# Two attention layers: packed third block for layer 2's keys and queries, shared image values for pairs of entries in layer 1

## The chip, the cores and the metric

The kernel runs on one core of a Trainium2 chip. The core has a matrix engine (PE, with its weight loads shown apart as PEld), a vector engine (DVE), a scalar engine (ACT), a general engine (POOL) and a queue engine (SP) that here issues nearly all DMAs. The metric is the device time of one execution in microseconds (us); lower is better. A profiled execution gives besides a trace of every instruction, whose times count from the first instruction (the span).

## The reference, cut to what matters

Sixteen entries (B = 16) of 256 query tokens with 320 channels pass through two cross-attention layers. Each attends to 256 context tokens of 512 channels. In layer 1 the first 77 are text and the other 179 are image tokens; in layer 2 the last 4 are image tokens and 252 are text. There are 20 heads of 16 channels.

```python
# layer 1 (layer 2 alike, with text = all but the last 4, and image scores by head)
text, ip = ctx[:, :77], ctx[:, 77:]
q, k_text, v_text = x @ Wq, text @ Wk, text @ Wv
logits = einsum("bhqd,bhkd->bhqk", heads(q), heads(k_text)) * scale
text_out = softmax(logits) @ heads(v_text)
ip_k, ip_v = ip @ Wk_ip, ip @ Wv_ip
scores = einsum("bhqd,bhkd->bhqk", heads(q), heads(ip_k)) * scale
...
ip_probs = softmax(scores + 0.5 * sem) * spatial_mask
out = (text_out + ip_probs @ heads(ip_v)) @ Wout + bout + x
```

## The kernel before, in words

**Numbers.** Every f32 operand is split into a high half, which the matrix engine takes exactly, and a low half, the remainder. `prod` (L255) makes a product of two split operands from three matmuls for each 128 rows of contraction: high by high, high by low, low by high. With 512 context channels that is 4 x 3 = 12 matmuls for one output block.

**Stages.** Layer 1 runs in 80 slots (16 entries x 5 groups of 4 heads; `slot0`, L810), then layer 2 in 80 slots (`slot1`, L993). A slot makes the scores of the group two ahead, the exponentials of its own and the weighted values of the group before. Between these stand fillers: the work of other entries (context, keys, queries, values, output projections), each a generator whose steps have a due time in slots in the table `STEPS` (L1186); `fill` (L1161) runs those that are due. PE follows the order in which this code issues in both layers; ACT, DVE and POOL do so in layer 2 and are put in order by the framework's scheduler in layer 1, as SP is in both.

**Keys and queries of layer 2.** `keys1` (L553) makes the keys in three blocks of 128 columns, `queries` (L636) with `project` (L626) the queries. There are 320 columns, so the weights are padded to 384 (24 columns for the 20 heads) and half of the third block is padding. High and low halves go to DRAM (`kd[1]`, `qd`) in three planes: for the keys low, high, high; for the queries high, low, high. `stacks1` (L747) loads them back for two heads at a time as stacks of 3 x 16 = 48 rows (`XROW`) on partitions 0 and 64 of the tiles `ks` and `qs`, so that one matmul with 48 rows of contraction makes all three products of a head's scores. Row 48 is used for the maximum that is subtracted (`KS1` = 49 rows). The loads are issued four slots ahead (`LEAD`), the scores made two slots ahead (`both1`, L903).

**Values of layer 1.** `values0_` (L423) makes, for each entry, three blocks of 128 tokens by 320 channels: t = 0, the text values of tokens 0 to 127; t = 1, the image values of the same tokens; t = 2, the image values of tokens 128 to 255. Of t = 0 and t = 1 the rows that don't belong are multiplied by zero when ACT moves the result to the value tile (`vr`, a ring of three, L429). In block t = 1 only the last 51 rows (tokens 77 to 127) count. The context of two entries is loaded and split together (`ct0`; tiles `cta` and `ctb`). `attend0` (L803) multiplies the value tiles with the probabilities.

**Order around the change.** SP issues in order: a DMA that waits holds up all that stand behind it. In layer 1 the stacks of a group can be loaded when PE is done with the group four before. In layer 2 the first stack of an entry waits for the keys' last block (`keys_out`, L347).

## Time and profile before

| | |
|---|---|
| median of 3 runs | 1475.77 us (1475.01 to 1476.06) |
| the profiled execution | 1477.49 us |
| its span, first to last instruction | 1475.7 us |
| PE busy | 1433.6 us (97%), 12438 matmuls |
| weight loads | 1186.7 us (80%) |
| DVE / POOL / ACT busy | 1166.0 (79%) / 1151.8 (78%) / 956.5 us (65%) |
| DMA | 211.78 MB, mean 144 GB/s |
| layer 1's scores, first to last | 44.0 to 645.9 us |
| layer 2's scores, first to last | 659.4 to 1430.4 us |

A row of the group list reads: line, engine, operation, what it writes and reads by the program's names, shapes, number, then busy time and the mean of one in nanoseconds, then the engine's idle time just before. A row of a timeline: start, duration, engine, line, operation. Matmuls overlap, so that the duration of one is longer than what it adds; what it adds is the distance to the next one's start. Issuing a DMA does not count as busy time; SP's issues stand in its timeline as SPq.

### The profile page before, as it was taken

What the parts mean: (1) busy time and instruction counts of PE and PEld (TensorE: products, weight loads), DVE (VectorE), ACT (ScalarE), POOL (GpSimd) and SP (SyncE); (2) the same over time, 40 slices, a digit from 0 to 9 for tenths busy, and PEclk for the clock granted to TensorE, in tenths of its full rate; (3) what the DMA queues carried; (4) which work ended last, traced back from release to release, by engine and by line L of the source; (5) the groups of instructions that cost most, each with busy time, mean ns of one, the idle gap of its engine ahead of it and who ended that gap; (6) DMA issues with size and microseconds to landing.
All of it is one profiled execution on the core that took longest, in us unless ns stands there. A gap on an engine that the chain in (4) does not pass through costs nothing.

```text
span 1475.7 us, 35302 instructions
## 1 busy us (share of the span) xinstructions
PE 1433.6 (97%) x12438; PEld 1186.7 (80%) x12438; DVE 1166.0 (79%) x2569; ACT 956.5 (65%) x2074; POOL 1151.8 (78%) x1173
## 2 busy tenths in 40 slices
PE   6899999999999999799999999999999999999998
PEld 6788888888888878687778887888888888888865
DVE  5487676777677787967888888888888888888897
ACT  5577676767676776756666566656665666566553
POOL 4179797979797877987788877787778877887785
PEclk9999999999999999999999999999999999999999
DMA  6756565656656577565434433543354345433511
GB/s 196 194 160 184 134 184 141 184 143 165 162 154 164 144 195 205 140 184 158 138 102 140 146 119 101 161 146 102 118 161 146 89 131 161 135 101 116 150 32 50
DMA packets 230667, 211.78 MB, mean 144 GB/s; under 512 B 56314, under 2 KB 217116, under 8 KB 230492
## 3 DMA queue, kind: packets, MB, share of 16 engines
q1 hardware_dynamic: 229222, 208.56, 50.3%
q8 instruction: 99, 1.62, 0.5%
q10 hardware_dynamic: 1270, 0.98, 0.2%
q14 instruction: 76, 0.62, 0.1%
HBM read 122.07 MB, written 86.44 MB: 141 GB/s over the span
## 4 chain that ended last, share of the span: by engine, by line
PE 86%; DMA 4%; DVE 3%; POOL 3%; ACT 2%; issue 1%; SPq 0%; ACTq 0%; DVEq 0%; POOLq 0%
PE X L260 22%; PE X L975 18%; PE X L632 11%; PE P L833 7%; PE S L772 5%; PE P L988 5%; PE T L917 5%; PE T L795 4%; PE S L922 3%; PE P L990 2%; DMA kd<-kst 2%; PE X L1108 1%; POOL P L801 1%; PE X L690 1%; POOL wt L966 1%
## 5 line engine op out<-in xcount | busy, mean ns | idle before, releaser
L801 POOL TENSOR_TENSOR P<-P,rs 128x512 f32<-128x512 f32 x320 | 413.6, 1316 | 140.2 <-ACT P L798 140.2
L975 PE MATMUL X<-ctb,gm 128*128 128x512 f32 x1120 | 295.3, 407 | 0.0
L966 POOL TENSOR_TENSOR wt<-P,ctb 128x512 f32<-128x512 f32 x212 | 268.6, 1296 | 0.0
L923 DVE TENSOR_REDUCE mn<-S 128x4 fp32r<-128x1008 f32 x160 | 192.8, 1205 | 81.0 <-PE S L922 79.4
L975 PEld LDWEIGHTS X<-ctb,gm 128*128 128x128 f32 x1120 | 203.6, 190 | 49.4 <-issue 0.4
L798 ACT ACTIVATE P<-T 128x512 f32<-128x512 f32 x320 | 174.7, 593 | 100.5 <-PE T L795 81.0
L978 DVE TENSOR_TENSOR wt<-X,wt 128x512 f32<-128x512 f32 x240 | 159.3, 681 | 4.9 <-PE X L975 4.9
L929 ACT ACTIVATE P<-T 128x512 f32<-128x512 f32 x212 | 115.0, 597 | 54.5 <-PE T L917 41.6
L980 POOL TENSOR_TENSOR wt<-wt 128x512 f32<-128x512 f32 x80 | 103.6, 1295 | 58.3 <-DVE wt L978 58.3
L965 ACT ACTIVATE ctb<-P 128x512 fp32r<-128x512 f32 x212 | 122.5, 625 | 32.7 <-PE X L975 31.1
L774 DVE TENSOR_REDUCE mn<-S 128x4 fp32r<-128x716 f32 x160 | 142.4, 890 | 0.0
L833 PE MATMUL P<-P,vr 128*32 128x256 f32 x1920 | 123.8, 387 | 1.8 <-DVE tmp L850 0.8
L632 PE MATMUL X<-hq,wE 128*128 128x256 f32 x768 | 111.1, 289 | 4.4 <-ACT hq L615 3.9
L260 PE MATMUL X<-cta,wA 128*128 128x252 f32 (+3 forms) x726 | 104.2, 289 | 6.9 <-ACT wA L187 6.8
L632 PE MATMUL X<-ho,wF 128*128 128x256 f32 x768 | 106.6, 284 | 0.9 <-DVE ho L871 0.6
L632 PEld LDWEIGHTS X<-hq,wE 128*128 128x128 f32 x768 | 101.6, 195 | 7.2 <-ACT hq L615 4.4
L260 PEld LDWEIGHTS X<-cta,wA 128*128 128x128 f32 (+1 forms) x726 | 94.4, 191 | 10.7 <-ACT wA L187 7.0
L632 PEld LDWEIGHTS X<-ho,wF 128*128 128x128 f32 x768 | 98.7, 189 | 3.9 <-DVE ho L871 1.0
L844 DVE STREAM_TRANSPOSE nt<-P 128x512 f32<-128x512 f32 x80 | 57.0, 713 | 44.2 <-PE P L833 43.9
L773 DVE TENSOR_REDUCE mn<-S 128x4 fp32r<-128x308 f32 x160 | 74.5, 466 | 21.5 <-PE S L772 21.1
L833 PEld LDWEIGHTS P<-P,vr 128*32 128x32 f32 x1920 | 55.7, 110 | 42.7 <-issue 6.0
L772 PE MATMUL S<-ks,qs 125*128 125x256 f32 x480 | 87.0, 304 | 0.9 <-DVE mn L774 0.8
(223 smaller groups left out, 3279.7 us busy)
## 6 DMA issues: line engine op xcount, KB each, us to landing
qd<-q SPq DMA_DIRECT2D x48, 384.0 KB
kd<-kst SPq DMA_DIRECT2D x66, 256.0 KB
rawc<-in_cT_dram SPq DMA_DIRECT2D x60, 256.0 KB
qs<-qd SPq DMA_DIRECT2D x160, 96.0 KB
ks<-kd SPq DMA_DIRECT2D x160, 96.0 KB
qs<-qd SPq DMA_DIRECT2D x60, 192.0 KB
ks<-kd SPq DMA_DIRECT2D x60, 192.0 KB
qd<-q SPq DMA_DIRECT2D x32, 256.0 KB
```

The source lines that it names most:

```text
L260: last = mm(out, lhs(a, k), rhs(b, k), start=i == 0, stop=i == len(terms) - 1)
L632: mm(pp, w(s, k, slice(m * 128, (m + 1) * 128)), a[:, t], start=i == 0, stop=i == len(terms) - 1)
L772: mm(sp[:, h], Q[: XROW + T0, h, t * 128 : (t + 1) * 128], K[: XROW + T0, h], start=True, stop=True)
L774: anchor(nc.vector.tensor_reduce(mn[:, t, 1], sp[:, :, T0:], axis=AX.X, op=ALU.max))
L798: exp = anchor(nc.scalar.activation(pt, st[p], AF.Exp, scale=SCALE))
L801: anchor(nc.gpsimd.tensor_mul(pt, pt, rs[:, t : t + 1].to_broadcast([128, 2, S])))
L833: mm(pv[32 * s : 32 * s + 32, o : o + S], v[:, vt, h : h + 32], P[k, s // 2][:, t, s % 2], start=vt < 2, stop=vt != 1,)
L923: anchor(nc.vector.tensor_reduce(maxes[k + 2][:, t], sp[:, :, :T1], axis=AX.X, op=ALU.max))
L965: nc.scalar.activation(R[k, u][:, t], P[k, u][:, t], AF.Copy, scale=0.5)
L966: anchor(nc.gpsimd.tensor_sub(W[k, u][:, t], P[k, u][:, t], f(R[k, u][:, t])))
L975: mm(yp, gm[:, gb], R[k, u][:, kt], start=i == 0, stop=i == len(blocks[n]) - 1)
L978: nc.vector.tensor_mul(product, yp, w[:, n])
```

## The change

**Layer 2's third block.** The weights are now packed to 320 columns without padding inside, and the 64 columns that are left over in the third block take the *low* halves of its 64 real columns (`lows_beside`). A product of these 128 columns' high part with both halves of the context (`both_halves`, 8 matmuls instead of 12) gives the real columns' main part on 64 rows and their correction on the other 64. For the queries (`project` with `beside`) it is 5 matmuls instead of 8. The correction is not added up: it goes to DRAM as extra rows, and a stack has 56 rows instead of 48 (`X1`), where main query by corrected key and corrected query by main key each have up to 4 rows. `weights8` writes zeros to the extra rows of heads that have none. Keys leave in 8 DMAs for an entry instead of 6 (`keys1_out`), queries in 7 instead of 3.

**Layer 1's shared values.** For the seven pairs of entries after the first, the 51 columns of image tokens of both entries are copied side by side to a tile `pair` (8 DVE copies of 128x102), one set of 12 matmuls makes the values of both (102 rows), ACT copies them to a tile `both`, and one DMA for each entry takes its 51 rows to partitions 77 to 127 of its value tile.

**Order.** In a slot of layer 2 the fillers due at 0.2 now come ahead of the first norm product, and `release`, which lets go of delayed work, one call earlier. Many due times in `STEPS` are different; two of its lines are shown.

```diff
 KS0 = 127
-KS1 = 49
+KS1 = 57
 XROW = 48
+X1 = 56
+LAST = slice(2 * 128, CQ)
+EXTRA = 3 * CQ
 
...
 
-    kd = [dram.tile([B // 2, 3, CQ, 2, S], F32, name="kd0"), dram.tile([B, 3, CP, 1, S], F32, name="kd1")]
+    kd = [dram.tile([B // 2, 3, CQ, 2, S], F32, name="kd0"), dram.tile([B, X1 * H, S], F32, name="kd1")]
+    qd1 = [dram.tile([X1 * H, S], F32, name=f"qd1{i}") for i in range(2)]
     vipd = dram.tile([BI, CP], F32, name="vipd")
...
-        w, parts, view = by_row(w_d, tag)
+    def lows_beside(w):
+
+        nc.gpsimd.tensor_copy(w[:, 0, :, CQ:], f(w[:, 1, :, LAST]))
+
+    def weights(w_d, tag, half=None, wait=0, raw="raw", beside=False):
+
+        w, parts, view = by_row(w_d, tag, beside)
         yield from in_turn(parts, wait, raw)
         if half is not None:
-            nc.vector.tensor_scalar_mul(w[:, 1, 2], f(w[:, 1, 2]), half)
+            n = CQ if beside else CP
+            nc.vector.tensor_scalar_mul(w[:, 1, 2, :n], f(w[:, 1, 2, :n]), half)
+        if beside:
+            lows_beside(w)
         return view
 
...
         return first, last
+
+    def both_halves(out, lhs, rhs, kt):
+
+        for k in range(kt):
+            for s in range(2):
+                mm(out, lhs(k), rhs(s, k), start=k + s == 0, stop=k + s == kt)
...
 
+    def keys1_out(d, m, kst):
+
+        hi, lo = kst[:, 0, 0], kst[:, 1, 0]
+        n, lo_row = min(CQ - m * 128, 128), m * 128
+        planes = d[:EXTRA].rearrange("(r c) t -> c r t", c=CQ)[lo_row : lo_row + n]
+        dma(planes[:, 1:], hi[:n].unsqueeze(1).to_broadcast([n, 2, S]))
+        dma(planes[:, 0], lo[:n])
+        if m == 2:
+            dma(d[EXTRA + H - 4 : EXTRA + 4 * H], hi[:64])
+            dma(d[EXTRA + 5 * H - 4 : EXTRA + 8 * H], hi[64:])
...
 
+    shared = {}
+
     def values0_(b):
         ct, i = ct0[b // 2], b % 2
         V = vr[(b + 2) % 3]
+        vc = vcols(V, V0W)
+        n = S // 2 - T0
+        if b > 1 and i == 0:
+            pair = buf("pair", [128, 4, 2, 2, n], FR)
+            for k in range(4):
+                for h in range(2):
+                    nc.vector.tensor_copy(pair[:, k, h], f(ct(h, k)[:, :, T0 : S // 2]))
+            pair = pair.rearrange("p k h b t -> p k h (b t)")
         for t, (w,), lo, sc in ((0, wv0, 0, tmask[:, 0:1]), (1, wvi0, 0, tmask[:, 1:2]), (2, wvi0, 128, 1.0)):
-            vp = bank()[:, :320]
-            prod(vp, lambda s, k: ct(s, k)[:, i, lo : lo + 128], lambda s, k: w(s, k), 4)
-            nc.scalar.activation(
-                vcols(V, V0W)[:, t, :, 0:16], vp.rearrange("p (h d) -> p h d", d=D), AF.Copy, scale=sc
-            )
+            if t != 1 or b < 2:
+                vp = bank()[:, :320]
+                prod(vp, lambda s, k: ct(s, k)[:, i, lo : lo + 128], lambda s, k: w(s, k), 4)
+                nc.scalar.activation(vc[:, t, :, 0:16], vp.rearrange("p (h d) -> p h d", d=D), AF.Copy, scale=sc)
+            else:
+                if i == 0:
+                    vp = bank()[: 2 * n, :320]
+                    prod(vp, lambda s, k: pair[:, k, s], lambda s, k: w(s, k), 4)
+                    shared[b // 2] = buf("both", [2 * n, 320])
+                    nc.scalar.copy(shared[b // 2], vp)
+                rows = shared[b // 2][i * n : (i + 1) * n]
+                dma(vc[T0:, 1, :, 0:16], rows.rearrange("p (h d) -> p h d", d=D))
...
-        image, wki1 = by_column(wki1_d)
-        _, text, w1["k"] = by_row(wk1_d, "wA")
+        image, wki1 = by_thirds(wki1_d)
+        wk, text, w1["k"] = by_row(wk1_d, "wA", True)
         yield from in_turn(image + text, 0.3, "rawc")
+        lows_beside(wk)
+        queued(nc.vector.memset(f(kip[64:, :, 2]), 0.0))
         for m in range(3):
-            kp = bank()[:, :BI]
-            prod(kp, lambda s, k: wki1(s, k, slice(m * 128, m * 128 + 128)), lambda s, k: cip[:, s, k], 4)
-            halves(kip[:, 0, m], kip[:, 1, m], kp)
+            n = min(CQ - m * 128, 128)
+            kp = bank()[:n, :BI]
+            prod(kp, lambda s, k: wki1(s, k, slice(m * 128, m * 128 + n)), lambda s, k: cip[:, s, k], 4)
+            halves(kip[:n, 0, m], kip[:n, 1, m], kp)
             yield
 
...
         nc.gpsimd.memset(f(zero), 0.0)
+        blank = zero[:16, :S].unsqueeze(1)
+        for d in (*(q.unsqueeze(0) for q in qd1), kd[1]):
+            for row in (EXTRA, EXTRA + 4 * H):
+                dma(d[:, row : row + 16].rearrange("b p t -> p b t"), blank.to_broadcast([16, d.shape[0], S]))
         yield
...
             kp = bank()[:, :T1]
-            prod(kp, lambda s, k: w1["k"](s, k, ms), lambda s, k: ct(s, k)[:, :T1], 4)
+            if m < 2:
+                prod(kp, lambda s, k: w1["k"](s, k, ms), lambda s, k: ct(s, k)[:, :T1], 4)
+            else:
+                both_halves(kp, lambda k: w1["k"](0, k, ms), lambda s, k: ct(s, k)[:, :T1], 4)
             nc.gpsimd.tensor_copy(kst[:, :, 0, T1:], f(kip[:, :, m, 4 * b : 4 * b + 4]))
             nc.scalar.copy(kst[:, 0, 0, :T1], kp)
             late(
                 lambda kst=kst, kp=kp: nc.vector.tensor_sub(kst[:, 1, 0, :T1], kp, f(kst[:, 0, 0, :T1])),
-                lambda kst=kst, m=m: keys_out(kd[1][b], m, kst),
+                lambda kst=kst, m=m: keys1_out(kd[1][b], m, kst),
             )
             yield
...
 
-    def project(l, w, a, evac):
+    def project(l, w, a, evac, beside=False):
 
         terms = [(s, k, t) for k in range(2) for s, t in ((0, k), (0, 3 + k), (1, k))] + [(0, 2, 2), (1, 2, 2)]
         for m in range(3):
             pp = bank()[:, :S]
-            for i, (s, k, t) in enumerate(terms):
-                mm(pp, w(s, k, slice(m * 128, (m + 1) * 128)), a[:, t], start=i == 0, stop=i == len(terms) - 1)
+            chain = [(0, k, t) for s, k, t in terms if s == 0] if beside and m == 2 else terms
+            for i, (s, k, t) in enumerate(chain):
+                mm(pp, w(s, k, slice(m * 128, (m + 1) * 128)), a[:, t], start=i == 0, stop=i == len(chain) - 1)
             evac(m, pp)
             yield
+
...
-        qd = dram.tile([3, (CQ, CP)[l], S], F32, tag=f"qd{l}", name=f"qd{l}", bufs=2)
+        yield from project(l, wq[l], a, evac, l == 1)
+        qd = qd1[len(opened) % 2] if l else dram.tile([3, CQ, S], F32, tag="qd0", name="qd0", bufs=2)
         settled()
         if l:
+            opened.append(qd)
+            planes = qd[:EXTRA].rearrange("(r c) t -> c r t", c=CQ)
             for r, s in ((0, 0), (1, 1), (2, 0)):
-                dma(qd[r].rearrange("(m p) t -> p m t", p=128), qh[:, s])
+                dma(planes[: 2 * 128, r].rearrange("(m p) t -> p m t", p=128), qh[:, s, :2])
+            dma(planes[LAST, ::2], qh[:64, 0, 2].unsqueeze(1).to_broadcast([64, 2, S]))
+            dma(planes[LAST, 1], qh[:64, 1, 2])
+            dma(qd[EXTRA + H - 4 : EXTRA + 4 * H], qh[64:, 0, 2])
+            dma(qd[EXTRA + 5 * H - 4 : EXTRA + 8 * H], qh[:64, 0, 2])
         else:
             for m in range(3):
...
         for u in range(2):
-            rows = slice(64 * u, 64 * u + XROW)
+            rows = slice(64 * u, 64 * u + X1)
             hs = slice(4 * g + u, 4 * g + u + 3, 2)
             if k - NS < n:
-                dma(K[64 * u + XROW : 64 * u + KS1], w1["ind"])
-            dma(K[rows], stack_rows(kd[1][b][:, :, 0])[:, hs])
-            dma(Q[rows], stack_rows(qd)[:, hs])
+                dma(K[64 * u + X1 : 64 * u + KS1], w1["ind"])
+            dma(K[rows], kd[1][b].rearrange("(d h) t -> d h t", h=H)[:, hs])
+            dma(Q[rows], qd.rearrange("(d h) t -> d h t", h=H)[:, hs])
 
     maxes, issues = {}, {}
...
         yield lambda: both1(k, 0)
+        yield release
         if k == NS:
             yield lambda: attend0(k - 1)
         summed = []
         if k > NS + 1:
             yield lambda: summed.append(attend1(k - 2))
-        yield release
         yield lambda: both1(k, 1)
+        yield 0.2
         if last:
             yield lambda: norm1(last, 0, 0)
-        yield 0.2
         for parts in summed:
             yield lambda: settle1(*parts)
         if last:
...
-        "k1": (-7, -6.2, -6.2, -5, -4.2, -3.4,),
+        "k1": (-7, -6.2, -6.2, -5.2, -4.2, -3.6,),
```

Three places show how instructions move; a row has the line, the operation, what is written and read with buffer numbers, and the shape.

**PE, layer 1, the second entry of a pair**, behind a slot's scores (`S`) and turned scores (`T`). Before: its image values t = 1 and t = 2 (`wD` are the image value weights; `cta` and `ctb` the context), then the next filler.

```order
L772 MATMUL S<-ks_190,qs_186 128x256 x4
L795 MATMUL T<-qs_188,ks_192 128x256 x4
L260 MATMUL X<-wD,cta_80 128x320 x3
L260 MATMUL X<-wD,cta_81 128x320 x3
L260 MATMUL X<-wD,ctb_82 128x320 x3
L260 MATMUL X<-wD,ctb_83 128x320 x3
L260 MATMUL X<-wD,cta_80 128x320 x3
L260 MATMUL X<-wD,cta_81 128x320 x3
L260 MATMUL X<-wD,ctb_82 128x320 x3
L260 MATMUL X<-wD,ctb_83 128x320 x3
L718 MATMUL X<-tph_448,M_332 128x256
```

And now:

```order
L836 MATMUL S<-ks_192,qs_188 128x256 x4
L859 MATMUL T<-qs_190,ks_194 128x256 x4
L271 MATMUL X<-wD,cta_82 128x320 x3
L271 MATMUL X<-wD,cta_83 128x320 x3
L271 MATMUL X<-wD,ctb_84 128x320 x3
L271 MATMUL X<-wD,ctb_85 128x320 x3
L782 MATMUL X<-tph_450,M_334 128x256
```

Twelve matmuls are gone; the first entry of the pair keeps its 24, the first twelve of which read `pair` now.

**SP, layer 1, around the new DMAs** (`xc` and `xq` are residual and input of an entry, `ks`/`qs` and `ksl`/`qsl` the ring of stacks). Before:

```order
L83 DMA ks_192<-kd_66 48x4x256
L83 DMA qs_188<-qd_1548 48x1024
L83 DMA xc_747<-in_xT_dram 128x3x256
L83 DMA ksl<-kd_66 48x4x256
L83 DMA qsl<-qd_1548 48x1024
L83 DMA xq_122<-in_xT_dram 128x3x256
```

And now:

```order
L86 DMA ks_194<-kd_66 48x4x256
L86 DMA qs_190<-qd_1548 48x1024
L86 DMA xc_749<-in_xT_dram 128x3x256
L86 DMA vr<-both 51x20x16 x2
L86 DMA ksl<-kd_66 48x4x256
L86 DMA qsl<-qd_1548 48x1024
L86 DMA xq_124<-in_xT_dram 128x3x256
```

The two value transfers of a pair stand between the residual's load and the next group's stacks. The first waits for ACT's copy to `both`, the second also for PE's last use of its value tile.

**SP, layer 2, from the last keys of an entry to its first stacks** (`kst` is the tile that keys leave from). Before:

```order
L83 DMA qs_187<-qd_15673 48x2x256 x4
L83 DMA qs_188<-qd_15673 48x2x256 x2
L83 DMA kd_67<-kst_235 128x2x256
L83 DMA kd_67<-kst_235 128x256
L83 DMA qs_188<-qd_15673 48x2x256 x2
L83 DMA ks_191<-kd_67 48x2x256 x4
```

And now:

```order
L86 DMA qs_189<-qd_68 56x2x256 x4
L86 DMA qs_190<-qd_68 56x2x256 x2
L86 DMA kd_67<-kst_237 64x2x256
L86 DMA kd_67<-kst_237 64x256 x3
L86 DMA qs_190<-qd_68 56x2x256 x2
L86 DMA ks_193<-kd_67 56x2x256 x4
```

The third block's keys leave in four DMAs of 64 rows instead of two of 128, in the same place, and each stack has 56 rows.

More of the change, by code (lines that the diff above doesn't have):

```diff
@@ L101, in buf @@
     def buf(tag, shape, dtype=F32, bufs=1, name=None):
-        if tag in ("wB", "wD", "vr", "raw"):
+        if tag in ("wB", "wD", "vr", "raw", "pair", "both"):
             return sb.tile(shape, dtype, tag=tag, name=name or tag, bufs=bufs)
@@ L232, in by_column @@
         )
-    def weights(w_d, tag, half=None, wait=0, raw="raw"):
-        w, parts, view = by_row(w_d, tag)
+    def lows_beside(w):
+        nc.gpsimd.tensor_copy(w[:, 0, :, CQ:], f(w[:, 1, :, LAST]))
+    def weights(w_d, tag, half=None, wait=0, raw="raw", beside=False):
+        w, parts, view = by_row(w_d, tag, beside)
         yield from in_turn(parts, wait, raw)
         if half is not None:
-            nc.vector.tensor_scalar_mul(w[:, 1, 2], f(w[:, 1, 2]), half)
+            n = CQ if beside else CP
+            nc.vector.tensor_scalar_mul(w[:, 1, 2, :n], f(w[:, 1, 2, :n]), half)
+        if beside:
+            lows_beside(w)
         return view
@@ L515, in weights2 @@
     def weights2():
-        wq.append((yield from weights(wq1_d, "wE", tmask[:, 3:4], 0.3, "rawc")))
+        wq.append((yield from weights(wq1_d, "wE", tmask[:, 3:4], 0.3, "rawc", True)))
     def weights4(l):
@@ L920, in both1 @@
                 for u in range(2):
-                    rows = slice(64 * u, 64 * u + XROW)
+                    rows = slice(64 * u, 64 * u + X1)
                     mm(sp[:, 2 * u + j], a[0][rows, j, t * 128 : (t + 1) * 128], a[1][rows, j], start=True, stop=True)
@@ L957, in maxima1 @@
         nc.scalar.copy(mt, mp[:4, :S])
-        row = QK[k][0].rearrange("(u p) j t -> u p j t", u=2)[:, XROW]
+        row = QK[k][0].rearrange("(u p) j t -> u p j t", u=2)[:, X1]
         late(lambda: nc.scalar.dma_start(f(row), f(mt)))
@@ L1225, in xattn2 @@
         ("c0", 1): (5.6, 6.4, 6.8, 7.8, 8.2, 9.2,),
+        ("q0", B - 2): tuple(NS + x for x in (-21.8, -21, -20, -19, -18,)),
+        ("q0", B - 1): tuple(NS + x for x in (-14.4, -14, -13, -12.8, -12,)),
+        ("m0t", B - 2): tuple(NS + x for x in (-17.4,)),
+        ("m0t", B - 1): tuple(NS + x for x in (-14.8,)),
+        ("v0", B - 2): tuple(NS + x for x in (-17, -15.4, -15,)),
+        ("v0", B - 1): tuple(NS + x for x in (-14, -13.8, -13.4,)),
+        ("s0", B - 2): tuple(NS + x for x in (-17.4, -16.4, -16, -15.4, -15, -14.4, -13.4,)),
+        ("s0", B - 1): tuple(NS + x for x in (-12.4, -11.4, -11, -10.8, -10.4, -10, -8.8,)),
+        ("c0", B - 2): (5.6, 6, 6.6, 7.2, 7.6, 8.2,),
     }
```

6 lines of the change are left out of this document (3 added, 3 removed), and 24 rows, old and new, of the table STEPS.

## The prediction

> **What bounds the kernel now.** I read three views in this order: the busy time of each engine in stretches of 80 us, the list of who waited for whom, and then the matrix engine's own timeline, from which the price of one matmul comes.
>
> ```profile
> core 0: us, PE busy (x) PEld busy (x) DVE busy (x) ACT busy (x) POOL busy (x), PEclk, DMA share, GB/s
> 320.00:400.00 80.00, 79.79 (x761) 68.62 (x760) 57.74 (x146) 58.61 (x130) 67.67 (x61) 1.00 0.60 157
> 560.00:640.00 80.00, 71.92 (x701) 59.64 (x699) 64.53 (x143) 55.39 (x116) 67.50 (x60) 0.96 0.63 165
> 640.00:720.00 80.00, 77.57 (x664) 62.64 (x662) 58.70 (x129) 46.98 (x104) 61.34 (x60) 0.98 0.51 153
> 1040.00:1120.00 80.00, 80.00 (x673) 64.82 (x672) 68.64 (x145) 50.50 (x112) 63.66 (x67) 1.00 0.39 114
> ```
>
> The columns behind the window are busy microseconds of PE, its weight loads, DVE, ACT and POOL, then the granted clock and the share of the DMA engines. The 320 row stands for layer 1, the 1040 row for layer 2, and the two between for the crossing from one to the other. In both layers PE works 79.8 to 80.0 of 80 us at a clock of 1.00. The next engine is POOL in layer 1 (67.7 of 80, 85%) and DVE in layer 2 (68.6 of 80, 86%). Only the crossing has PE time to spare: 8.1 us in the one row and 2.4 in the other.
>
> ```profile
> PE X L260 <- ACT wA L187: 7.0, 3, 5.1
> PE T L795 <- DMA qs<-mt: 4.6, 1, 4.6
> PE S L922 <- DVE sr L939: 2.3, 4, 0.8
> PE P L833 <- POOL P L801: 0.2, 1, 0.2
> PE 86%; DMA 4%; DVE 3%; POOL 3%; ACT 2%; issue 1%; SPq 0%; ACTq 0%; DVEq 0%; POOLq 0%
> ```
>
> The first four rows are waits of PE (total us, times, longest): the two largest come once or three times, at the start. The busiest partner in layer 2, DVE behind the scores, kept PE for 2.3 us in 4 places in all, and POOL's products in layer 1 kept it for 0.2 us. The last row is the chain that ended last: 86% of it is PE. So in both layers a matmul that is left out shortens the run by the time from its start to the next one's start, until an engine at 85 or 86% becomes the limit; that is far off for a cut of some 2%.
>
> **The change part by part.** The price of a matmul is not its mean duration in the list of groups (they overlap) but the distance between starts:
>
> ```profile
> 1031.10 1.55 PE L260 MATMUL X<-cta,wA 128*128 128x252 f32 x12
> 1032.48 0.86 PE L975 MATMUL X<-ctb,gm 128*128 128x512 f32 x3
> 1011.08 1.11 PE L632 MATMUL X<-hq,wE 128*128 128x256 f32 x8
> 1012.03 2.49 PE L975 MATMUL X<-ctb,gm 128*128 128x512 f32 x10
> 325.40 1.05 PE L260 MATMUL X<-wD,cta 128*128 128x320 f32 x6
> 327.17 1.04 PE L260 MATMUL X<-wD,cta 128*128 128x320 f32 x6
> ```
>
> Start, duration, then the group. Twelve key products of layer 2 (252 columns) take 1032.48 - 1031.10 = 1.38 us, 115 ns each. Eight query products (256 columns) take 0.95 us, 119 ns each. Twelve value products of layer 1 (320 columns; the other six stand between these two rows) take 1.77 us, 147.5 ns each.
>
> *Keys of layer 2.* Block m = 2 goes from 12 matmuls to 8 (the low halves of its 64 weight columns lie in columns that held padding, so one pass serves both). 4 x 16 entries x 115 ns = 7.4 us less.
> *Queries of layer 2.* Block m = 2 goes from 8 to 5. 3 x 16 x 119 ns = 5.7 us less.
> *Shared image values of layer 1.* Seven pairs do twelve products once instead of twice: 7 x 12 x 147.5 ns = 12.4 us less.
> Sum on PE: 25.5 us less, 13.1 of it in layer 2.
>
> What is added lies on other engines:
>
> ```profile
> L939 DVE COPY sr<-S 128x16 f32<-128x16 f32 x160 | 26.1, 163 | 0.0
> L564 DVE TENSOR_TENSOR kst<-X,kst 128x252 fp32r<-128x252 f32 x48 | 18.5, 387 | 1.4 <-ACT kst L562 1.4
> L429 ACT ACTIVATE vr<-X,tmask 128x320 f32<-128x320 f32 x32 | 17.0, 530 | 18.5 <-PE X L260 17.9
> ```
>
> *Gathering the pair.* 56 DVE copies of 128x102, a size that the trace doesn't show. Between the 128x16 copy (163 ns) and the 128x252 subtraction (387 ns) lie 9.1 and 21.7 us; I take 0.25 us each, 14 us, because 102 is nearer to 16 than to 252. DVE idles 22 of 80 us in layer 1, so I cost them at nothing. Without that cover it would be 14 us, and the products of the pair would start late. A gain from them is excluded: they replace nothing.
> *ACT.* 14 evacuations become 7 plain copies: some 7 x 0.53 = 3.7 us less on an engine that isn't the bound. Nothing.
> *The values' way to their tile.* 14 new DMAs of 51 rows by 20 pieces of 64 bytes, on SP's queue right ahead of a load of key and query stacks. The second of each two also waits until PE has attended the last group of the tile's former owner, and behind it on SP stand those stack loads. What they can afford is seen here:
>
> ```profile
> 326.97 0.39 SPq L83 DMA_DIRECT2D xc<-in_xT_dram  x1
> 333.90 0.31 SPq L83 DMA_DIRECT2D ksl<-kd  x1
> 334.26 0.43 SPq L83 DMA_DIRECT2D qsl<-qd  x1
> 344.83 0.69 PE L772 MATMUL S<-ksl,qsl 125*128 125x256 f32 x4
> ```
>
> SP stands idle from 327.36 to 333.90, until PE has freed the stack, and the new DMAs fall into that gap. From the end of the stack's issue (334.69) to its first score are 10.1 us. A write with its issue done at 1038.22 had let its readers go at 1040.69 (rows below), so a landing takes at most 2.5 us and 7.6 us are to spare. The new transfer itself has no row. From below I take that landing, 2.5 us; from above four times it, 9.9 us, since 51 x 20 = 1,020 pieces are four times the 256 of such a key write. The upper end costs 2.3 us of PE a pair, 16 us in all; the lower end nothing. I take nothing, because a piece of 64 bytes is a sixteenth of a 1 KB one.
> *SP in layer 2.* Two more key DMAs and four more query DMAs an entry. The tight place is the first stack of an entry:
>
> ```profile
> 1037.33 0.89 SPq L83 DMA_DIRECT2D kd<-kst  x2
> 1038.31 0.87 SPq L83 DMA_DIRECT2D qs<-qd  x2
> 1040.69 4.06 SPq L83 DMA_DIRECT2D ks<-kd  x8
> 1046.06 0.51 PE L922 MATMUL S<-ks,qs 48*128 48x256 f32 x4
> ```
>
> One issue takes about 0.45 us (0.89 for two). The third block's keys leave in four DMAs instead of two: 0.9 us later. The two loads of the first stack are out by 1041.7, land by 1044.2, and its scores start at 1046.06: 1.9 us to spare, so 0.9 us is hidden, and the larger loads (112 KB for 96) a little more. The four query DMAs are earlier in the queue, ahead of waits that SP has anyway. If none of it were hidden: 6 x 0.45 = 2.7 us an entry, 43 us in all; from below nothing. I take nothing, from the 1.9 us.
> *Order and setup.* Fillers now come ahead of the first norm product of a slot, the times of many fillers are changed, weights are packed, and six DMAs write zeros. In the layers PE has no idle time that an order could give or take. In the crossing it is 10.5 us in two rows: so up to 10 us of gain, or as much loss; I take nothing, having no row for either.
>
> The sum is 25.5 us. The profiled execution took 1477.49 us with a span of 1475.7, and the median of the runs is 1475.77: from 1477.49 it gives 1452, from the median **1450**.
>
> **The rivals.**
> *Half of it only.* One layer keeps its pace because another chain sets it: DVE in layer 2 (68.6 of 80 us busy; with 1.7% less PE time 87%), or the DVE copies uncovered in layer 1. It would leave 12.4 or 13.1 us of gain, 1463. Against it speak the 2.3 us of waits above.
> *More than the sum.* The new filler times also close the crossing's idle time: up to 10 us more, 1440. For it speak 8.1 us of idle time in one row; against it, that the work which crosses there is the same.
> *The new value transfers hold up the stacks: slower.* Suppose that a transfer of 51 = 3 x 17 rows is not spread over all DMA engines but held by three of them. The price then comes from this row:
>
> ```profile
> q1 hardware_dynamic: 229222, 208.56, 50.3%
> ```
>
> 229,222 packets took 50.3% of 16 engines' 1475.7 us: 52 ns on the mean. 1,020 pieces on 16 engines are 64 each, 3.3 us, hidden; on three they are 340 each, 17.7 us at that mean. That is 10.1 us past the 7.6 to spare, seven times: 71 us lost, 25.5 won, 1521. It decides from 7.6 + 25.5 / 7 = 11.2 us for a transfer, which is 33 ns a piece on three engines. Against it speaks that the mean packet has 910 bytes and these have 64, so I expect far less than 33 ns. The Trainium skill has such a rule (DMA: Bandwidth & Descriptors, "Why a DMA increments its semaphore by 16 and not by 1"): a transfer runs on the largest number of engines up to 16 that divides the outermost sizes on both sides, which for 51 is 3 and for the new 56-row stacks 14. No row of this trace shows it.
> *The change does not do what it says.* The order of the changed program shows 64, 48 and 84 matmuls fewer, so this falls away.
>
> **How the numbers follow.** Full sum 68% (1445 to 1457), half 13%, more than the sum 10%, value transfers or another late DMA making it slower 7%, no change 2%. The time is that of the likeliest, 1450. The range takes in the crossing's 10 us below and the uncovered copies' 14 us above: 1440 to 1464, which leaves out the slower case and the edges of two others, under 2 in 10. About 0.2% is what a measurement of this kernel can tell from no change: faster 0.90, same 0.03, slower 0.07.
>
> **What would show it.** Right: PE's instruction count in an 80 us row stays near 673 to 761 with PE at 79 to 80 us busy, the distances of 115, 119 and 147 ns stand, an entry of layer 2 is 0.8 us shorter and a pair of layer 1 1.8 us, and the stretch before the first scores is unchanged. Wrong: waits of PE on DMA for the stacks of layer 1 (value transfers) or for the first stack of each entry in layer 2 (SP's queue); DVE near 80 of 80 in layer 2; or crossing rows with PE several us busier or idler than 71.9 and 77.6. If the sum was right and the time is not near 1450, the difference must stand in the crossing's rows.

## The result, and the profile after

The changed kernel takes 1482.93 us (median of 6 runs, 1482.15 to 1489.23) where the kernel before took 1475.91 on the same chip: a ratio of 1.0052, 95% interval 1.0034 to 1.007. It is slower by 7 us; the forecast was 1450, faster by 25.5, and the range ended at 1464. The profiled execution took 1483.4 us with a span of 1481.6.

First the busy time of the engines on the page of the changed kernel, and the row of its chain that ended last:

```profile
PE 1415.4 (96%) x12242; PEld 1163.8 (79%) x12242; DVE 1207.0 (81%) x2627; ACT 955.0 (64%) x2068; POOL 1147.9 (77%) x1175
PE 72%; DVE 11%; DMA 7%; POOL 3%; issue 2%; ACT 2%; SPq 2%; ACTq 0%; DVEq 0%; POOLq 0%
```

The 196 matmuls are gone (12,438 before) and PE is busy 18.2 us less. But DVE is busy 41 us more, and of the chain PE now makes 72% where it made 86%; DVE's share went from 3 to 11%, the DMAs' from 4 to 7%.

The same four stretches as in the prediction, with the same columns (busy us of PE, weight loads, DVE, ACT, POOL; granted clock, DMA share, GB/s):

```profile
320.00:400.00 80.00, 77.94 (x739) 66.75 (x732) 63.89 (x151) 56.54 (x124) 66.51 (x60) 1.00 0.61 156
560.00:640.00 80.00, 64.18 (x618) 52.41 (x614) 57.96 (x131) 49.08 (x109) 56.48 (x54) 0.91 0.67 163
640.00:720.00 80.00, 74.85 (x652) 61.30 (x644) 57.51 (x125) 46.19 (x99) 64.27 (x63) 0.96 0.62 172
1040.00:1120.00 80.00, 79.89 (x673) 64.42 (x665) 69.59 (x148) 50.64 (x110) 62.55 (x70) 1.00 0.51 145
```

Layer 2 (the last row) is as full as before, 79.9 of 80 us. Layer 1 has lost 1.9 us of PE in 80, and the crossing 7.7 and 2.7, beside a granted clock of 0.91 for 0.96 in its first row.

Where the time goes is seen best from the start of each group's first score matmul (160 groups, five for each entry in either layer), changed kernel minus kernel before, in us. Such starts are read from PE's timeline, and the later tables are made in the same way:

| group | 10 | 20 | 30 | 40 | 50 | 60 | 65 | 70 | 75 | 85 | 100 | 120 | 140 | 155 | end |
|---|---|---|---|---|---|---|---|---|---|---|---|---|---|---|---|
| after - before | -1.4 | -0.7 | -0.1 | 0.6 | 1.2 | 1.9 | 6.1 | 12.4 | 16.0 | 15.9 | 15.4 | 11.8 | 8.6 | 6.8 | 5.9 |

Three parts. Layer 1 to group 60 is 1.9 us later, though six pairs had shared their products by then, which should give 6 x 1.77 = 10.6. The crossing (60 to 85) loses 14.0. Layer 2 wins 8.6 from group 100 to 155, 11 entries: 0.78 us an entry, where 13.1 / 16 = 0.82 was forecast. (The other runs with the packed block win 0.53 to 0.73 an entry there; what takes the rest is not shown.)

Four waits of PE in the changed kernel (total us, times, longest) that are longer than they were:

```profile
PE X L844 <- DVE mn L838: 9.2, 8, 1.5
PE P L897 <- ACT P L862: 6.3, 1, 6.3
PE X L773 <- ACT sp L769: 6.2, 2, 5.8
PE S L836 <- DVE mn L838: 4.3, 6, 0.9
```

And what the kernel before has of them:

```profile
PE X L780 <- DVE mn L774: 3.7, 4, 1.4
PE X L709 <- ACT sp L705: 3.4, 2, 2.9
PE S L772 <- DVE mn L774: 0.8, 1, 0.8
```

The first and the last row of the changed kernel are waits for the maximum of the scores, made by DVE. Between 130 and 490 us, in four pairs, they sum to 7.5 us, where the kernel before has none; the first half of a pair loses 2.2 us there. The second row is one stall in the crossing, which the kernel before does not have.

The copies that I had costed at 0.25 us, in the list of the tile's instructions (nanoseconds: shortest, median, longest):

```profile
L462 DVE CAST pair<-cta x28: 197/1047/1349, 52.9 to 501.2; 128x102 fp32r<-128x102 f32 x28
L462 DVE CAST pair<-ctb x28: 191/998/1262, 60.8 to 511.2; 128x102 fp32r<-128x102 f32 x28
```

The same instruction takes 0.19 us at best and 1.0 in the median; all 56 take 50.2 us. What a long one waits for is seen beside POOL. DVE's timeline of the changed kernel, and after it POOL's in the same stretch (start, duration):

```profile
195.77 1.04 DVE L462 CAST pair<-cta 128x102 fp32r<-128x102 f32 x1
196.73 0.47 DVE L959 SCALAR_TENSOR_TENSOR xc<-X,bo,xc 128x256 f32<-128x256 f32 x1
197.13 1.35 DVE L462 CAST pair<-cta 128x102 fp32r<-128x102 f32 x1
```

```profile
194.18 2.57 POOL L192 TENSOR_TENSOR cta<-rawc,cta 128x512 fp32r<-128x512 f32 x2
196.69 0.48 POOL L919 TENSOR_TENSOR hsn<-tmp 128x128 f32<-128x128 f32 x1
197.11 5.05 POOL L865 TENSOR_TENSOR P<-P,rs 128x512 f32<-128x512 f32 x4
```

The first copy starts inside a POOL instruction that ends at 194.18 + 2.57 = 196.75, and ends at 196.81. The second starts just behind the beginning of four POOL instructions of 5.05 / 4 = 1.26 us, the first of which ends near 198.4, and ends at 198.48. So it goes for the long copies, 49 of the 56: each ends some 0.07 us after a POOL instruction that ran when it started. The instruction between them (L959, which reads PE's accumulator X and one tile of the on-chip memory, xc) is not held: 0.47 us, as elsewhere.

The Trainium skill has this (SBUF — State Buffer, "Who interferes with whom"): DVE shares one pair of memory ports with POOL as an exclusive lock; copies from this memory to itself in a two-port mode, and DVE instructions with two operands from it, take part in the lock, reductions don't. The trace agrees for the copies: 0.19 us free, 1.0 us beside POOL. That rule spoke against the change, and the prediction did not weigh it.

The chain of the same stretch (start, duration, what; rows between are left out) shows what the copies cost:

```profile
195.77 1.04 DVE pair L462
197.13 1.35 DVE pair L462
198.81 0.62 DVE nt L908
202.56 0.92 DVE pair L462
205.40 0.98 DVE pair L462
207.00 0.63 DVE pair L462
207.63 0.39 DVE mn L837
208.02 0.82 DVE mn L838
208.88 0.23 PE X L844
```

But for some 1.5 us of issue, all of this chain from 195 to 208.9 us is DVE's; then PE goes on. DVE idles in layer 1 on the average, but a pair's eight copies all fall into one stretch of 16 us, between the reductions of the scores that PE waits for, and there DVE had become the bound.

### The profile page after: what moved, and what is told of

Its sections match the earlier page's. It is cut to its first block, busy times and chain, and to the rows that moved or that the text cites. A ratio compares the mean times of both kernels' runs of the same rounds, so it can differ in the third digit from the quotient of the medians.

```text
span 1481.6 us, 35178 instructions
## 1 busy us (share of the span) xinstructions
PE 1415.4 (96%) x12242; PEld 1163.8 (79%) x12242; DVE 1207.0 (81%) x2627; ACT 955.0 (64%) x2068; POOL 1147.9 (77%) x1175
## 4 chain that ended last, share of the span: by engine, by line
PE 72%; DVE 11%; DMA 7%; POOL 3%; issue 2%; ACT 2%; SPq 2%; ACTq 0%; DVEq 0%; POOLq 0%
PE X L271 17%; PE X L1039 16%; PE X L688 8%; PE P L897 5%; PE P L1052 4%; PE S L836 4%; PE T L981 4%; PE T L859 3%; PE S L986 3%; DVE pair L462 2%; PE P L1054 2%; DMA kd<-kst 2%; SPq L86 2%; DVE mn L838 2%; DMA qs<-qd 2%
## 5 line engine op out<-in xcount | busy, mean ns | idle before, releaser
L1039 PE MATMUL X<-ctb,gm 128*128 128x512 f32 x1120 | 291.4, 405 | 0.0
L688 PE MATMUL X<-ho,wF 128*128 128x256 f32 x768 | 110.3, 287 | 1.7 <-DVE ho L937 0.7
L688 PE MATMUL X<-hq,wE 128*128 128x256 f32 x720 | 105.8, 290 | 4.8 <-ACT hq L670 3.7
L688 PEld LDWEIGHTS X<-hq,wE 128*128 128x128 f32 x720 | 95.1, 195 | 7.9 <-ACT hq L670 4.2
L836 PEld LDWEIGHTS S<-ks,qs 125*128 125x128 f32 x480 | 66.0, 193 | 31.1 <-issue 20.0
L837 DVE TENSOR_REDUCE mn<-S 128x4 fp32r<-128x308 f32 x160 | 73.8, 461 | 20.3 <-PE S L836 19.7
L271 PE MATMUL X<-cta,wA 128*128 128x252 f32 (+3 forms) x534 | 78.3, 292 | 7.8 <-ACT wA L191 5.6
```

Of the source, the lines that this page charges most:

```text
L271: last = mm(out, lhs(a, k), rhs(b, k), start=i == 0, stop=i == len(terms) - 1)
L688: mm(pp, w(s, k, slice(m * 128, (m + 1) * 128)), a[:, t], start=i == 0, stop=i == len(chain) - 1)
L836: mm(sp[:, h], Q[: XROW + T0, h, t * 128 : (t + 1) * 128], K[: XROW + T0, h], start=True, stop=True)
L1039: mm(yp, gm[:, gb], R[k, u][:, kt], start=i == 0, stop=i == len(blocks[n]) - 1)
```

## The experiments

The expectations name five theories. **P**: the DVE copies wait for POOL and eat up what layer 1 should gain. **Q**: the shared products or their transfers cost it instead. **Z**: the six writes of zeros disturb the crossing. **V**: the value transfers do. **T**: the new due times do. Each ratio is against the kernel before, run beside it on the same chip. SBUF, in the expectations, is the on-chip memory.

**First set: one part at a time.** The pair gathered on ACT instead of DVE:

```diff
-                    nc.vector.tensor_copy(pair[:, k, h], f(ct(h, k)[:, :, T0 : S // 2]))
+                    nc.scalar.copy(pair[:, k, h], f(ct(h, k)[:, :, T0 : S // 2]))
```

> The pair is gathered by ACT instead of DVE, nothing else. Theory P (the DVE copies of 128x102 take 0.9 us in place of 0.2 because each waits until a running POOL instruction ends; DVE then reads the scores late and PE waits): the copies take about 0.3 us, layer 1 up to its 60th group of heads is some 10 us shorter than before the change where the changed kernel was 1.9 us longer, and the whole is about 12 us under the changed kernel, near 1471. Rival Q (the shared products themselves or their transfers cost what they win): layer 1 stays at the changed kernel's pace, and the time within 2 us of 1483.

Measured: 1508.93 us, ratio 1.022 (1.0203 to 1.0237). A miss: the copies took 0.28 us on ACT, and yet layer 1 lost 7 to 8 us in one half of most pairs. What held it is seen in reduce_copies below.

The changed kernel without the shared values (`if b > 1 and i == 0` and `if t != 1 or b < 2` made false and true), and the kernel before with the shared values alone:

> The changed kernel without the shared values: every entry makes its own three value blocks as before; the packed third block and the new times stay. Theory P: layer 1 is at the old pace (60th group within 1 us of before), layer 2 0.8 us an entry shorter. For the crossing, theory Z (the zeros and the larger DMAs around them hold up the stack loads): the 14 us loss of the crossing stays, and the whole is some 1475 to 1481. Theory V (the value transfers in the crossing hold them up): the crossing loses under 5 us, and the whole is about 1465.

> The kernel before with the shared values alone (DVE copies), old times, no packed block. Theory P: layer 1 loses some 2 us in seven pairs, and without the zeros and the new times the crossing loses little (theory Z or times): 1476 to 1482. Theory V: the crossing loses some 10 us more: 1486 to 1492. If the copies cost nothing: 1463.

Measured: no_share 1478.89 us, 1.0017 (1.0006 to 1.0029); share_only 1486.24 us, 1.0069 (1.0054 to 1.0084). Without sharing, layer 1 stays exactly 1.0 us ahead of the kernel before from group 10 to 60; with sharing alone it falls back to 4.8 us behind at group 60 and ends 9.8 late. So the sharing, meant to save 12.4, costs about 10 by itself, and about 5 beside the other changes (1.0052 against 1.0017). Of P's range for share_only (1476 to 1482) that is a miss: its layer 1 lost 4.8 where some 2 were expected, and its crossing 5.0. And no_share still loses 9 us in the crossing (from -1.0 at group 60 to 8.1 at 85): a loss that is not of the sharing.

The changed kernel with the due times of before (`STEPS` of before):

> The changed kernel with the old due times of the fillers. Theory T (the new times make the crossing's loss): some 10 us under the changed kernel, near 1472. Theories Z and V: the crossing's loss of 14 us stays within 4 us, and the time within 5 us of 1483.

Measured: 1483.84 us, 1.0058 (1.0036 to 1.008). The total is that of the changed kernel, so the new times are not what made it slower. They only move the loss: with the old ones the crossing loses 8.7 us instead of 14.0 (5.3 at group 60, 14.0 at 85), outside the 4 us of the expectation, and layer 1 loses 3.4 more. PE's stall of 6.3 us on ACT's exponentials is not in its list of waits either, so that stall takes the new times as well as the zeros (below). As the cause of the slower total, T falls.

**Second set: the copies.** The gathers by a DVE reduction over one element, at the same places:

```diff
-                    nc.vector.tensor_copy(pair[:, k, h], f(ct(h, k)[:, :, T0 : S // 2]))
+                    nc.vector.tensor_reduce(pair[:, k, h], f(ct(h, k)[:, :, T0 : S // 2]).unsqueeze(3), axis=AX.X, op=ALU.max)
```

> The changed kernel with the 56 gathers of the pair done by DVE as a maximum over one element (TENSOR_REDUCE) instead of a copy; DVE's list is otherwise the same, POOL's and PE's are the same. Theory P (a DVE copy from SBUF to SBUF waits for the end of the POOL instruction that runs, a reduction does not): the gathers take 0.2 to 0.35 us instead of 0.9 to 1.05, the score groups of layer 1 keep the pace that the products left out give them (group 60 starts 8 to 11 us before its start in the kernel before, instead of 1.9 after), and the time falls by 8 to 12 us to 1471 to 1475. Theory Q (the shared products, their transfers and their bank cost layer 1 what it gained, whatever the copies take): gathers short or not, group 60 stays within 3 us of the kernel before and the time at 1480 to 1486.

The kernel before with the copies into a tile that nobody reads, all products kept:

```diff
+        if b > 1 and i == 0:
+            pair = buf("pair", [128, 4, 2, 2, S // 2 - T0], FR)
+            for k in range(4):
+                for h in range(2):
+                    nc.vector.tensor_copy(pair[:, k, h], f(ct(h, k)[:, :, T0 : S // 2]))
```

> The kernel before, all its products kept, with the 56 DVE copies of the pair added into a tile that nobody reads. Theory P: the copies take about 1 us each, delay the score reductions behind them on DVE, and layer 1 loses what it lost between the products' gain and the measured pace: group 60 starts 8 to 13 us later than before, the time is 1484 to 1490. Theory Q: the copies are hidden in DVE's idle time, group 60 within 2 us, time 1475 to 1478.

Measured: copies_alone 1485.7 us, 1.006 (1.0043 to 1.0076), 6.5 us late at group 60 and 9.0 at 65. Eight copies a pair cost 9.4 us by layer 2, with nothing else changed. That the copies delay PE is as P said, and so is the time, but the 6.5 lie under its 8 to 13 for group 60: from group 20 to 60 a pair loses 0.9 us, not the 2.4 by which the changed kernel's pairs fall short of their gain. And reduce_copies took 1505.78 us, 1.0194 (1.0174 to 1.0214). Its gathers, in the list of the tile's instructions:

```profile
L462 DVE TENSOR_REDUCE pair<-cta x28: 235/252/260, 52.8 to 524.7; 128x102 fp32r<-128x102 f32 x28
```

All are short, with POOL beside them or not. And the gain of the products appears: from group 15 to 20, 25 to 30, 35 to 40 it wins 1.8 us each, the 12 x 147.5 ns of the prediction. But in the first half of a pair it loses 7 to 8 (4.7 in the first pair from group 10 on). DVE's timeline of reduce_copies, then POOL's:

```profile
209.12 0.42 DVE L914 TENSOR_TENSOR tmp<-nt,P 128x256 f32<-128x256 f32 x1
209.45 7.33 DVE L673 SCALAR_TENSOR_TENSOR hq<-hq,tmask,xq 128x256 fp32r<-128x256 f32 x1
216.71 0.37 DVE L757 TENSOR_TENSOR sp<-sp,X 128x77 f32<-128x77 f32 x2
217.00 0.47 DVE L837 TENSOR_REDUCE mn<-S 128x4 fp32r<-128x308 f32 x1
```

```profile
207.36 5.06 POOL L865 TENSOR_TENSOR P<-P,rs 128x512 f32<-128x512 f32 x4
212.36 1.30 POOL L671 TENSOR_TENSOR hq<-xq,hq 128x512 fp32r<-128x512 f32 x1
213.61 0.46 POOL L919 TENSOR_TENSOR hsn<-tmp 128x128 f32<-128x128 f32 x1
214.02 2.49 POOL L865 TENSOR_TENSOR P<-P,rs 128x512 f32<-128x512 f32 x2
```

The low half of the queries (L673), 0.43 us at best, lasts 7.33: it ends 0.28 us after the last of a row of POOL instructions that follow each other without a gap (214.02 + 2.49 = 216.51), and the score reduction L837 stands behind it. It reads two tiles of the on-chip memory. By the Trainium skill (SBUF — State Buffer, "Who interferes with whom") such an instruction takes part in the lock as well; the trace agrees, with 7.33 us for 0.43. L914 just before it starts beside POOL too, but reads one of its operands from the accumulator (`P` there), and it takes 0.42; in the changed kernel it takes 0.39 to 0.42 in all 80 places. In act_copies L673 lasted 7.38 to 7.40 us in most pairs. That is why both missed: shorter gathers moved the other locked instruction to a place where POOL did not let it in.

So L673 was taken off DVE, from the fourth entry on, as a subtraction on POOL of the 64 rows where the mask isn't zero:

```diff
-            third()
+            order(eng.tensor_sub(hl[64:, 2], src[64:, 2], f(hl[64:, 2])))
```

> The kernel of reduce_copies, with the third low half of the layer-1 queries (hq) no longer made by a DVE instruction with two SBUF operands but by a POOL subtraction on its 64 rows. In reduce_copies the gathers took 0.25 us as theory P says, and the second half of each pair gained the 1.8 us of the products left out, but the first half lost 8 us: the DVE instruction on hq, 0.43 us elsewhere, lasted 7.33 us, to 0.28 us past the end of a row of POOL instructions, and the scores waited 5.3 us behind it. Theory P, widened (every DVE instruction that takes part in the port lock with POOL can be held, not copies alone): without it no such wait of 5.3 us is left, group 60 of layer 1 starts 7 to 11 us before its start in the kernel before, and the time is 1470 to 1476. Theory Q (something else in the shared products costs layer 1): the loss of some 8 us a pair stays, 1495 to 1510, or group 60 comes out within 3 us of the kernel before and the time at 1479 to 1486. A risk of its own is POOL, 85% busy in layer 1, which gets some 0.7 us an entry more.

> The changed kernel with the gathers left as DVE copies and only the layer-1 subtraction on hq moved to POOL, as in short_and_hq: the fourth corner beside after (copies, hq on DVE), reduce_copies (reductions, hq on DVE) and short_and_hq (reductions, hq on POOL). Theory P: the copies still take about 1 us, so group 60 starts 0 to 5 us after its start in the kernel before and the time is 1481 to 1488; the 12 us that short_and_hq gained over the changed kernel come from the gathers. If they came from the subtraction alone: 1470 to 1474, with group 60 some 6 us before its start in the kernel before.

Measured: short_and_hq 1471.38 us, 0.9965 (0.9952 to 0.9977); hq_sub, with the copies kept, 1476.63 us, 1.0005 (0.9995 to 1.0015), outside both cases of its expectation and between them. The time of short_and_hq is as expected, its 6.5 us at group 60 a little short of the 7 to 11.

| start minus before, group | 10 | 20 | 30 | 40 | 50 | 60 | 85 | end |
|---|---|---|---|---|---|---|---|---|
| short_and_hq | -2.8 | -3.0 | -3.9 | -4.8 | -5.7 | -6.5 | 4.1 | -6.6 |
| hq_sub | -0.9 | -0.0 | -0.5 | -0.9 | -1.3 | -1.7 | 8.5 | -1.0 |

With neither lock in the way layer 1 gains 0.9 us a pair (1.8 in one half, 0.9 given back in the other). Where it gives back, PE waits once a pair for POOL, which has the subtraction now. In the whole run (the last number is the longest; in the pairs from 130 to 490 us it is 0.2 each):

```profile
PE P L897 <- POOL P L865: 3.4, 11, 0.6
```

The kernel before has one such wait of 0.2 us. Such a wait doesn't make 0.9, and the rest is not shown. The copies alone make the difference of 5.3 us between the two kernels. The rest of the 12 us between the changed kernel and short_and_hq came with the subtraction's move, which theory P had not foreseen: DVE's list is in another order then, and only 43.9 us are spent in copies. How much of that is L673 itself and how much the order was not separated.

**Third set: the crossing.** The zeros written in the middle of layer 1, from a tile of their own that waits for the values of entry 6; in no_share, and together with the edits above:

```diff
-        for d in (*(q.unsqueeze(0) for q in qd1), kd[1]):
-            for row in (EXTRA, EXTRA + 4 * H):
-                dma(d[:, row : row + 16].rearrange("b p t -> p b t"), blank.to_broadcast([16, d.shape[0], S]))
...
+        nc.gpsimd.tensor_scalar_mul(blank, f(results["v0", 6][:16, 0, :S]), 0.0)
...
+    task(("w9",), [26 + 2 * i for i in range(7)], blanks, ("v0", 6))
```

> The changed kernel without the shared values, and with the six writes of zeros issued in the middle of layer 1 instead of right ahead of the crossing. Nothing else moves but SP's order there, which becomes that of the kernel before (three writes of spread_d, x1d, one more, then the loads ks and qs). Theory Z (the crossing loses because the zeros push the writes of spread_d up to the loads of the last stacks): the wait of 7.3 us at 563 to 570 us goes, score group 80 starts 0 to 2 us before its start in the kernel before instead of 6.5 after, and the time falls by 7 to 9 us to 1469 to 1472. Rival W (the packed weights and their larger loads cost the crossing itself, not the zeros): group 80 stays 5 us or more late and the time at 1477 to 1480.

Measured: 1469.91 us, 0.9954 (0.9939 to 0.9969). The wait of 7.3 us is gone and group 80 starts 0.7 us before its start in the kernel before (no_share: 6.5 after). Z holds: the crossing's loss from group 60 to 85 falls from 9.1 to 2.8 us. The trace says how. ACT's timeline of no_share, then of zeros_early:

```profile
558.74 0.78 ACT L808 CAST ks<-M 77x716 fp32r<-77x716 f32 x1
568.77 0.62 ACTq L847 DMA_DIRECT2D qs<-mt  x1
569.50 1.08 ACT L862 ACTIVATE P<-T 128x512 f32<-128x512 f32 x2 [9.98 <-DMA qs<-qd]
```

```profile
558.68 0.78 ACT L813 CAST ks<-M 77x716 fp32r<-77x716 f32 x1
559.08 0.62 ACTq L852 DMA_DIRECT2D qs<-mt  x1
559.81 1.09 ACT L867 ACTIVATE P<-T 128x512 f32<-128x512 f32 x2 [0.35 <-ACT ks L813]
```

ACT issues the write of a group's maxima (`qs<-mt`) itself. In no_share that issue waits 10 us for the load of another group's stack, and the exponentials stand behind it. SP's timeline of no_share has that load:

```profile
558.62 1.42 SPq L86 DMA_DIRECT2D spread_d<-kb  x2
560.13 1.08 SPq L86 DMA_DIRECT2D ks<-kd  x1
561.26 1.25 SPq L86 DMA_DIRECT2D qs<-qd  x1
```

It leaves hardly later than in the kernel before (560.58 us there). Why the maxima wait for it at all stands in the lists of the two programs, which name the completion counters, DMAHW0 to DMAHW7, that a DMA waits for:

```
no_share     SP   L86 DMA qs0_188<-qd0_6953 48x1024   [waits DMAHW2_49]
             ACT  L847 DMA qs2_190<-mt_0_198 2x4x256  [waits DMAHW2_49,Activation_49]
zeros_early  SP   L86 DMA spread_d_71<-kb_0_240 128x4x384  [waits DMAHW1_49]
             ACT  L852 DMA qs2_190<-mt_0_198 2x4x256  [waits DMAHW1_49,Activation_49]
```

In both lists the eight counters serve all 1,451 DMAs in strict turn, and these maxima wait for the DMA eight places ahead, which had their counter. Six DMAs more shift the turn, and the maxima of buffer 2 come to stand behind the load of buffer 0, issued 2.4 us after they are ready and landing 7.5 us later; in zeros_early they stand behind a write of `spread_d` that left before. So it is not, as my expectation had it, that the loads are pushed back, but whose turn the maxima share. No run moved the turn alone. The changed kernel itself has the same pair of DMAs on one counter, and ACT waits as long:

```profile
576.36 1.09 ACT L862 ACTIVATE P<-T 128x512 f32<-128x512 f32 x2 [8.97 <-DMA qs<-qd]
```

> The changed kernel with both: the pair gathered by reductions, and the zeros written in the middle of layer 1. If P and Z both hold, layer 1 gains 8 to 11 us, the crossing keeps them, and layer 2 gains its 8 to 12: 1452 to 1463, faster than the kernel before. If only P holds 1471 to 1475; if only Z, 1473 to 1476; if neither, 1480 to 1486. Theory V (the value transfers still cost the crossing some 5 us beside the zeros) puts it at 1460 to 1468.

> The kernel of short_and_hq with the zeros written in the middle of layer 1 as in zeros_early. If theory P as widened and theory Z both hold: 7 to 11 us from layer 1 on top of the 6.4 us that zeros_early gained, 1458 to 1464. If only Z: 1470 to 1476. If the value transfers still cost the crossing: 1463 to 1468.

> The control for all_three: the kernel of zeros_early (packed third block, zeros in the middle of layer 1, no shared values), with the subtraction on POOL alone. It says what that edit is worth by itself: within 2 us of zeros_early (1468 to 1472) if DVE's instruction on hq cost nothing there (it lasted 0.43 to 0.49 us in nearly all entries), some 3 us slower if POOL is the one that is short.

Measured: both_fixes (reductions and early zeros, L673 left on DVE) 1501.62 us, 1.0162 (1.014 to 1.0184): layer 1 loses as in reduce_copies, 26.3 us at group 60, outside every case of its expectation, which was written before that loss was known. all_three 1468.11 us, 0.9936 (0.9915 to 0.9956); zeros_and_hq, the same without sharing, 1472.9 us, 0.9976 (0.9961 to 0.9992). From group 60 to 80 both lose 4.8 us alike, so the value transfers add nothing to the crossing there: V falls. The sharing is worth 4.8 us between these two, where 12.4 was forecast. The subtraction on POOL has a price of its own: zeros_and_hq is 3.0 us over zeros_early, as its expectation said for a POOL that is short. all_three missed its 1458 to 1464: its layer 1 gains 2.9 us by group 60 where short_and_hq gained 6.5, which the runs don't explain. It has the lowest time here and is faster than the kernel before and than the changed one; zeros_early, the smaller edit, cannot be told from it (the intervals overlap).

## Why the prediction was wrong, step by step

**PE as the bound** was right of the kernel before, and the **prices of a matmul** held where PE stayed the bound: 0.78 us an entry in layer 2 of the changed kernel for 0.82, and 1.8 us a pair in layer 1 (reduce_copies, second halves).

**The price of the copies** failed first. I put 0.25 us between two rows, a copy of 128x16 (163 ns) and a subtraction of 128x252 (387 ns). Both read the matrix engine's accumulator (`S`, `X`), not the on-chip memory on both sides; they were the nearest rows in size, not in kind. The median was 1.0 us, above my upper end. The trace of before had rows of the right kind:

```profile
L1060 DVE SCALAR_TENSOR_TENSOR u<-u,tmp x17: 215/939/1011, 748.3 to 1461.3; 128x40 f32<-128x40 f32 x15, 128x32 f32<-128x32 f32 x1, 128x8 f32<-128x8 f32 x1
L618 DVE SCALAR_TENSOR_TENSOR hq<-hq,tmask,xq x32: 429/488/1517, 19.2 to 1349.4; 128x256 fp32r<-128x256 f32 x32
```

Both read two tiles of the on-chip memory. One takes 0.94 us for 40 elements, more than twice the 0.387 of the subtraction of 252 elements that reads only one; the other takes from 0.43 to 1.52 for one shape. Such instructions wait after their start.

**"DVE idles 22 of 80 us, so I cost them at nothing"** failed with it. The average over 80 us did not say whether the idle time lies where the copies go. The step should have asked what DVE does in the 16 us between the splitting of the pair's context and its products, and who waits for it there: PE, for the score maxima. Instead of -10.6 us by group 60 the changed kernel has +1.9. The runs part these 12.5 us so: 3.6 go with the move of L673 off DVE and the other order that it brings (hq_sub), 4.8 with the copies (short_and_hq), and 4.1 are still missing in short_and_hq, which stays open. The rival *half of it only* had named uncovered copies, but as a gain that is lost; it had no loss in it.

**"Order and setup: nothing, up to 10 us either way"** failed too. The crossing cost 14.0 us from group 60 to 85. Of these 4.9 come with the sharing (no_share loses 9.1; copies_alone loses 2.7 there, so part of it is the copies', and the rest was not separated), 6.3 with the zeros, and 2.8 are left in zeros_early, with the packed block and the new times. So order and setup proper cost 9.1, near the 10 that the step allowed for; to take nothing was the error. I had counted the zeros as six DMAs without asking past which queue entries and counters they move the others.

**The values' way** and **SP in layer 2**, both taken as nothing, were nothing: no wait of PE on the value tile's transfers or on an entry's first stack stands in PE's list of waits, and layer 2 wins most of what its matmuls are worth. The rival with 17.7 us a transfer did not come true. That its chance of 7% for "slower" covered the right sign was luck: the reason was another. The range's upper end, 14 us for uncovered copies, was their time by the wrong price; they took 50.2.

## What to carry to other kernels

A DVE instruction that copies within the on-chip memory, or reads two operands from it, had no price of its own here while POOL was busy: it ended when POOL's instruction ended, or later. Where such a price is needed, look in the trace for instructions of the same kind whose longest is several times their shortest, put one operand in the accumulator, or use a reduction. Time that an engine idles covers new work only if it lies between the same two events; and a DMA added to a program is an entry in a turn that others share, not only bytes.

## What was not expected of the hardware

The hold is not always one POOL instruction long. In the changed kernel the instruction on `hq` got in when the current one ended (0.73 us in four pairs), as all held copies did; in reduce_copies it waited out the rest of that one and six more (7.33 us, until POOL ran dry, the same in four pairs, and 4.2 and 4.5 us in two others). The section of the Trainium skill named above has the other side blocked for the whole instruction; these runs show a block over seven. What decides whether DVE gets in at a boundary is open. So is the clock: the stretch from 560 to 640 us shows 0.91 in the changed kernel and in no_share, which have a PE stall of 6 to 7 us there, and 0.96 in the kernel before and in zeros_early, which have none so long; but old_times, whose longest wait of PE there is 3.6 us, shows 0.91 too. What lowers it is not shown.
